# Two key tiles of an attention kernel written as one pattern of TensorE work

## The chip, the cores and the metric

The kernel runs on one core of a Trainium2 chip. The metric is the device time of one execution in microseconds. The kernel before took 3696.45 us in the median of three runs (3693.88 to 3697.93). All times below are in microseconds unless they are marked otherwise.

## What is computed

The reference is one transformer block with four batches of 2048 rows and 256 features, everything in float32. Attention has 16 heads of 16 features; the feed-forward part has 704 hidden features, and its activations and weights are quantized to FP4 in blocks of 16 and multiplied out again.

```
q, k, v = heads(x @ Wq.T), heads(x @ Wk.T), heads(x @ Wv.T)
scores  = einsum('bhld,bhmd->bhlm', q, k) * SCALE
out     = einsum('bhlm,bhmd->bhld', softmax(scores), v)
x = layernorm(x + merge(out) @ Wo.T)
h = silu(fp4(x) @ fp4(w_gate).T) * (fp4(x) @ fp4(w_up).T)
x = layernorm(x + fp4(h) @ fp4(w_down).T)
```

## The kernel before, in words

Attention is cut into 64 steps: batch, block of 512 queries (QB), and group of four heads (`steps`, line 351). A step walks over 16 tiles of 128 keys (NKT), and each such tile of one step is a period, so there are 1024 of them. The main loop (line 700) counts periods in `n`, with 20 more in front (LEAD) and 2 behind (LAG).

In one period the loop hands out this work, and `matmul` and `transpose` (lines 133 to 137) keep TensorE in the order in which it is written:

- `maxima` (line 382), for the step that is 20 periods ahead: for each pair of heads two matmuls of 62 rows into a two-bank PSUM tile `pm` (two buffers), then one VectorE reduction `mx` over both (line 397). They find the maximum of each query's scores, which the exponentials later subtract.
- `exponentials` (line 423), for the present step: for each pair of heads two matmuls `pe` of 64 rows, each into a bank from `psum` (line 106), then two ScalarE exponentials `e` (line 431). The even head lies on rows 0 to 63 of the array, the odd head on rows 64 to 127. The 64 rows are 16 features in a split of high and low parts, with two rows for the maximum.
- `values` (line 434), for the tile two periods back: four matmuls that the compiler makes into eight, `av`, 32 columns of the array for each head.
- `period` (line 654): it runs the steps that have fallen due (`take_due`, line 122), one part of each generator in `urgent`, and then parts of the first generator in `queue` until one with a cost of at least LEAST (300) has been run (two such parts before the first exponentials). A cost is a number that a generator yields; it serves to count parts alone.

The order in a period is: both maxima, first pair of exponentials, values, second pair of exponentials, then the part.

The banks that `psum` gives out are three, used in turn by the exponentials and by every part. `urgent` holds `max_rows` (line 399), which reduces the maxima of a finished step, pauses twice, transposes them (`pn`), copies them with ScalarE (`nr`) and has SyncE's queue write them into the last two rows of the query tiles with four DMAs (line 418); and `normalize` (line 448), which copies the finished `av` with ScalarE, pauses twice, transposes it (`pa`), divides it, and for every second step transposes the result (`pr`). `queue` holds everything else in parts: the projections of the next batch (`project`, line 300, tiles `ptx`, `pq`, `pv`), the quantized weights (`prepare`, line 232), and for each finished query block `chain` (line 673) with `feed_forward` (line 585): `residual` (`py`), `gated` (`pg`, `pu`), `turned` (`pth`) and `down` (`pz`). A generator that has to wait for something yields LEAST without any work, and the part of that period is empty.

Loads of keys, queries and values (`load_k`, `load_q`, `load_v`, lines 354 to 380) go through SyncE's queue. Keys are loaded in blocks of 512 keys, two tiles per block, seven blocks ahead of the exponentials, into 20 buffers (line 369).

When the main loop is over, `banks["more"]` lets `psum` use the banks of the maxima as well, and the rest of the queue runs with one part in each `period` (line 739).

Of the kernel before, what the change touches and what calls it, by code (L numbers as in the profile page):

```python
# [28 lines left out]
F32 = mybir.dt.float32  # L32
F32R = mybir.dt.float32r
# [5 lines left out]
P = 128  # L39
# [12 lines left out]
LN_EPS = 1e-5  # L52
LEAD = 20
LAG = 2
LEAST = 300.0
PSUM = bass.MemoryType.PSUM
DRAM = bass.MemoryType.DRAM
# [16 lines left out]
def block_kernel(  # L74
# [58 lines left out]
    def matmul(*args, **kw):  # L133
        tc.keep_in_program_order(nc.tensor.matmul(*args, **kw))  # L134
# [97 lines left out]
    def prepare():  # L232

        raw = p2.tile([P, KC, D], F32, tag="wl", name="wo", bufs=1)
        nc.sync.dma_start(raw, wo.rearrange("(c p) k -> p c k", p=P))
        yield 0
        pt = psum("ptw")
        for kc in range(KC):
            for n in range(KC):
                at = (kc * KC + n) * P  # L240
                transpose(pt[:, at : at + P], raw[:, n, kc * P : (kc + 1) * P], ident)
        nc.scalar.copy(woT.rearrange("p k n -> p (k n)"), pt)
        yield 500

        def load(w, i):
            if w is w_down:
                t = p2.tile([P, FF], F32, tag="wl", name="wl", bufs=1)
                nc.sync.dma_start(t, w[i * P : (i + 1) * P, :])
                return fp4(p2, t.rearrange("p (b f) -> p b f", f=FB), "h")
            t = p2.tile([RF, 2, D], F32, tag="wl", name="wl", bufs=1)  # L250
            nc.sync.dma_start(t, w[2 * i * RF : 2 * (i + 1) * RF, :].rearrange("(c p) k -> p c k", p=RF))
            return fp4(p2, t.rearrange("p c (b f) -> p (c b) f", f=FB), "")

        def transposed(w, i, q, done):
            while not done():
                yield LEAST
            if w is w_down:
                q = q.rearrange("p b f -> p (b f)")
                for c0 in range(0, NFC, 4):
                    pt = psum("ptw")  # L260
                    for c in range(c0, min(c0 + 4, NFC)):
                        n = min(P, FF - c * P)
                        at = (c - c0) * P
                        transpose(pt[:n, at : at + P], q[:, c * P : c * P + n], ident)
                        nc.scalar.copy(wdT[:n, c, i * P : (i + 1) * P], pt[:n, at : at + P])
                return
            q = q.rearrange("p (c b) f -> p c (b f)", c=2)
            pt = psum("ptw")
            for kc in range(KC):
                for c in range(2):  # L270
                    at = (2 * kc + c) * RF
                    transpose(pt[:, at : at + RF], q[:, c, kc * P : (kc + 1) * P], ident[:RF, :RF])
            dst = wgT if w is w_gate else wuT
            nc.scalar.copy(
                dst[:, :, 2 * i * RF : 2 * (i + 1) * RF], pt[:, : 4 * RF].rearrange("p (k n) -> p k n", k=KC)
            )

        pieces = [(w, i) for w in (w_gate, w_up) for i in range(4)] + [(w_down, i) for i in range(KC)]
        q = load(*pieces[0])
        yield 1  # L280
        for piece, after in zip(pieces, pieces[1:] + [None]):
            following = load(*after) if after else None
            yield from transposed(*piece, *q)
            q = following
            yield 500

    def weave(main, other, k):

# [11 lines left out]
    def project(b, tb, what):  # L300
# [7 lines left out]
        for kc in range(KC):  # L308
            pt = psum("ptx")
            for t in range(QT):  # L310
                transpose(pt[:, t * P : (t + 1) * P], xb[:, t, kc * P : (kc + 1) * P], ident)
            nc.scalar.copy(xT[:, kc, :], pt)
            yield 600
        for name, c in [(w[0], int(w[1])) for w in what if w != "v"]:
            w, dst = (wkT, kx[b % 2][c][:, :, rows]) if name == "k" else (wqT, qx[(b * NQB + tb) % len(qx)][c])
            hi = p2.tile([P, QB], F32R, tag="hi", name=name + "hi", bufs=3)
# [48 lines left out]
    def load_k(s, kb):  # L365
        b, qb, g = steps[s]
        for i in range(NP):
            c, h = divmod(g * HG + i * 2, NC)
            k = p1.tile([P, QB], F32R, tag="k", name="k", bufs=20)
            for j in range(2):  # L370
                nc.sync.dma_start(
                    k[R * j : R * j + R, :].bitcast(F32), kx[b % 2][c][:, h + j, kb * QB : (kb + 1) * QB]
                )
            k_sb[s, i, kb] = k
# [45 lines left out]
                )  # L420
        yield 400

    def exponentials(s, kt, i):
        kb, col = kt // QT, kt % QT * P
        pe = [psum("pe") for _ in range(2)]
        for j in range(2):
            rows = slice(R * j, R * j + R)
            matmul(pe[j], k_sb[s, i, kb][rows, col : col + P], q_sb[s, i][rows, :], start=True, stop=True)
        for j in range(2):
            e = p1.tile([P, QB], F32, tag="e", name="e", bufs=10)  # L430
            nc.scalar.activation(e, pe[j], AF.Exp, scale=SCALE)  # L431
            e_sb[s, kt, 2 * i + j] = e

    def values(s, kt):
        if kt == 0:
# [12 lines left out]
    def normalize(s):  # L448

        av_sb = p2.tile([P, QB], F32, tag="av_sb", name="av_sb", bufs=1)  # L450
        nc.scalar.copy(av_sb, av_ps.pop(s))
        yield 0
        yield 0
        pa = psum("pa")
        for t in range(QT):
            transpose(pa[:, t * P : (t + 1) * P], av_sb[:, t * P : (t + 1) * P], ident)

        pairs = pa.rearrange("p (t i a d) -> p t i a d", t=QT, i=NP, d=DH)
        rd = p2.tile([P, QT, NP, 2], F32, tag="rd", name="rd")
        nc.vector.reciprocal(rd, pairs[:, :, :, 1:3, 0])  # L460
        if s % 2 == 0:
            oq_of[s // 2] = p2.tile([P, QT, P], F32, tag="oq", name="oq", bufs=1)
        oq = oq_of[s // 2].rearrange("p t (g i j d) -> p t g i j d", g=2, i=NP, d=DH)
        for i in range(NP):
            nc.vector.tensor_tensor(
                oq[:, :, s % 2, i],
                pairs[:, :, i, 0:4:3, :],
                rd[:, :, i, :].unsqueeze(3).to_broadcast([P, QT, 2, DH]),
                ALU.mult,
            )  # L470
        yield 500
        if s % 2 == 0:
            return
        yield 0
        pr = psum("pr")
        for t in range(QT):
            transpose(pr[:, t * P : (t + 1) * P], oq_of[s // 2][:, t, :], ident)
        oT = p1.tile([P, QB], F32, tag="oT", name="oT", bufs=3)
        nc.scalar.copy(oT, pr)
        oTs[s // 2] = oT  # L480
        yield 500


    def layer_norm(r, t0, n):
# [69 lines left out]
    def turned(hq, tiles, hT):  # L554
# [4 lines left out]
        for t in range(2):  # L559
            pt = psum("pth")  # L560
            for c in range(4):
                transpose(pt[:, c * P : (c + 1) * P], hq[t][:, c * P : (c + 1) * P], ident)
            nc.scalar.copy(hT[:, t, :4, :].rearrange("p c n -> p (c n)"), pt)
            yield 500
        pt = psum("pth").rearrange("p (t c n) -> p t c n", t=2, c=2)
        for t in range(2):
            for c in range(4, NFC):
# [2 lines left out]
        for c in range(4, NFC):  # L570
            w = min(P, FF - c * P)
            nc.scalar.copy(hT[:w, :, c, :], pt[:w, :, c - 4, :])
        yield 500

    def down(x1, hT, t):
        for n in range(KC):
# [8 lines left out]
    def feed_forward(b, qb, between):  # L585
# [14 lines left out]
        for kc in range(KC):  # L600
            pt = psum("ptq")
            for t in range(QT):
                q = xq[t // 2][0].rearrange("p (t b) f -> p t (b f)", t=2)
                transpose(pt[:, t * P : (t + 1) * P], q[:, t % 2, kc * P : (kc + 1) * P], ident)
            nc.scalar.copy(xqT[:, kc, :], pt)
            yield 500
        hq = {}

        def gate(t):
# [41 lines left out]
                q.popleft()  # L651
        return None

    def period(parts):

        take_due()
        for _ in range(len(urgent)):
            cost = next(urgent[0], None)
            if cost is not None:
# [1 line left out]
            urgent.popleft()  # L661
            parts -= (cost or 0.0) >= LEAST
        while parts > 0 and queue:
            parts -= (part(queue) or 0.0) >= LEAST

    def projection(b, tb, what=("k0", "q0", "v", "k1", "q1")):
        return project(b, tb, what)
# [29 lines left out]
    others = [projection(0, tb, ("q0", "q1")) for tb in range(1, NQB)] + [projection(1, 0)]  # L697
    queue.append(weave(prepare(), chain_of(others), 2))

    for n in range(-LEAD, N + LAG):  # L700
        m = n + LEAD
        (sm, im), (s, kt), (sv, kv) = divmod(m, NKT), divmod(n, NKT), divmod(n - LAG, NKT)
        if m in (8, 10, 12, 14):
            if m == 8:
                load_q(1)
# [13 lines left out]
                assert (b, kb // QT, "k" + c) in projected  # L719
                load_k(ahead, kb // QT)  # L720

        for i in range(NP):
            if m < N:
                maxima(sm, im, i)
        for i in range(NP):
            if 0 <= n < N:
                exponentials(s, kt, i)
            if i == 0 and n >= LAG:
                values(sv, kv)
        if m < N and im == NKT - 1:  # L730
            urgent.append(max_rows(sm))
        if n >= LAG and kv == NKT - 1:
            urgent.append(normalize(sv))
            if sv % NG == NG - 1:
                queue.append(chain(*steps[sv][:2]))
        period(1 if n >= 0 else 2)
    banks["more"] = True
    while urgent or queue or due:
        period(1)

# [1 line left out]
_INS = [  # L744
    "L0_attn_x",
# [29 lines left out]
```

## Time and profile before

The profile is that of one execution, which took 3695.37 us by its own measurement; its span, from the first instruction to the last, is 3693.6 us. That lies 1.1 us under the median of the runs.

| what | value |
|---|---|
| median of three runs | 3696.45 us |
| the profiled execution's own time | 3695.37 us |
| its span | 3693.6 us |
| mean granted TensorE clock | 0.982 |
| `mx` reductions on VectorE | 2048, busy 2407.9 us, mean 1217 ns |
| `e` exponentials on ScalarE | 4096, busy 2217.9 us, mean 595 ns |
| `av` matmuls | 8192, busy 1098.3 us |
| `pe` matmuls | 4096, busy 1037.2 us |
| `pm` matmuls | 4096, busy 803.8 us |
| ScalarE idle before `e`, waiting for `pe` | 666.0 us |
| VectorE idle before `mx`, waiting for `pm` | 702.5 us |

A row of the profile names the engine, the line of the kernel, the operation, the tile that is written and those that are read, and how often it was executed. PE is TensorE's matmul, PEld its weight load, DVE is VectorE, ACT ScalarE, POOL GpSimd, and SPq SyncE's DMA queue. The timeline gives start, length and operation; instructions of one kind that follow each other are merged into one row. [...] lengths overlap and the distance of two starts says more. Behind `<-` stands what ended the idle time before a row.

### The profile page before, as it was taken

How to read it: one execution, taken by the hardware profiler on the slowest of the kernel's cores; microseconds unless marked ns; L12 is line 12 of the kernel's file. 1: busy time of each engine (PE TensorE's matmuls, PEld its weight loads, DVE VectorE, ACT ScalarE, POOL GpSimd, SP SyncE). 2: the span in 40 equal slices, each digit the busy share in tenths (PEclk: the TensorE clock that was granted, in tenths of full speed). 3: DMA queues.
4: the chain of work that ended last, by engine and by line, in shares of the span. 5: the costliest groups of instructions: out<-in, count | busy, mean ns of one | idle time of the engine just before them, and what ended most of it. 6: DMA issues, size and time to landing. Idle time of an engine off the chain costs nothing.

```text
span 3693.6 us, 57860 instructions
## 1 busy us (share of the span) xinstructions
PE 3540.7 (96%) x21396; PEld 1602.0 (43%) x21396; DVE 2805.0 (76%) x3250; ACT 2694.0 (73%) x5452; POOL 1293.4 (35%) x1542
## 2 busy tenths in 40 slices
PE   5889999999999999999999999999999999999995
PEld 4433444444444444444444444444443434444343
DVE  3777777787787877878787787778778788878834
ACT  2667777777777777777777777777777777777772
POOL 0331432424243242423424243342424325241425
PEclk8899999999999999999999999999999999999997
DMA  6643333223232332323323232322322221222100
GB/s 217 188 137 117 93 91 105 81 85 115 68 114 84 94 94 85 109 70 109 95 78 106 85 97 88 97 89 74 113 75 63 75 79 57 75 68 86 47 7 6
DMA packets 197954, 334.18 MB, mean 90 GB/s; under 512 B 26024, under 2 KB 75560, under 8 KB 197672
## 3 DMA queue, kind: packets, MB, share of 16 engines
q1 hardware_dynamic: 196280, 329.16, 29.2%
q8 instruction: 171, 2.80, 0.3%
q10 hardware_dynamic: 1392, 1.31, 0.1%
q14 instruction: 111, 0.91, 0.1%
HBM read 242.81 MB, written 86.51 MB: 89 GB/s over the span
## 4 chain that ended last, share of the span: by engine, by line
PE 82%; DVE 11%; DMA 2%; POOL 2%; SPq 1%; issue 1%; ACT 1%; ACTq 0%; POOLq 0%; DVEq 0%
PE av L134 24%; PE pe L134 18%; PE pm L134 16%; DVE mx L397 8%; PE pz L134 5%; PE pg L134 5%; PE pu L134 5%; PE pq L134 3%; PE pth L137 1%; PE pv L134 1%; PE pa L137 1%; PE py L134 1%; PE pn L137 1%; DMA k<-kx 1%; DMA xb<-in_L_attn_x_dram 1%; DVE amax L149 1%
## 5 line engine op out<-in xcount | busy, mean ns | idle before, releaser
L397 DVE TENSOR_REDUCE mx<-pm 128x2 f32<-128x1024 f32 x2048 | 2407.9, 1217 | 706.8 <-PE pm L134 702.5
L431 ACT ACTIVATE e<-pe 128x512 f32<-128x512 f32 x4096 | 2217.9, 595 | 671.2 <-PE pe L134 666.0
L134 PE MATMUL av<-e,v 128*32 128x512 f32 x8192 | 1098.3, 608 | 0.0
L134 PE MATMUL pe<-q,k 64*128 64x512 f32 x4096 | 1037.2, 456 | 4.8 <-ACT e L431 4.4
L134 PEld LDWEIGHTS pe<-q,k 64*128 64x128 f32 x4096 | 476.4, 185 | 969.0 <-ACT e L431 855.7
L134 PE MATMUL pm<-k,q 62*128 62x512 f32 x4096 | 803.8, 448 | 60.0 <-DVE mx L397 53.0
L134 PEld LDWEIGHTS pm<-k,q 62*128 62x128 f32 x4096 | 347.0, 186 | 373.2 <-issue 178.6
L134 PEld LDWEIGHTS av<-e,v 128*32 128x32 f32 x8192 | 162.2, 108 | 332.2 <-issue 314.1
L537 POOL TENSOR_TENSOR a<-a,g 128x352 f32<-128x352 f32 x124 | 116.4, 939 | 499.5 <-ACT a L536 499.5
L582 POOL TENSOR_TENSOR x<-x,read 128x128 f32<-128x128 f32 x128 | 58.9, 460 | 493.6 <-ACT read L142 493.6
L134 PE MATMUL pz<-wdT,hT 128*128 128x128 f32 (+1 forms) x1536 | 230.0, 292 | 0.0
L163 POOL TENSOR_TENSOR xn<-xn,m 128x704 f32<-128x704 f32 (+2 forms) x104 | 159.5, 1534 | 157.7 <-DVE m L162 139.0
L134 PEld LDWEIGHTS pz<-wdT,hT 128*128 128x128 f32 (+1 forms) x1536 | 191.0, 191 | 45.5 <-ACT e L431 18.2
L551 POOL TENSOR_TENSOR h<-a,u 128x352 f32<-128x352 f32 x124 | 116.2, 937 | 226.7 <-ACT u L550 224.4
L134 PE MATMUL pg<-wgT,xqT 128*128 128x352 f32 x512 | 187.4, 489 | 0.0
L513 POOL TENSOR_TENSOR x<-x,read 128x256 f32<-128x256 f32 x64 | 46.7, 730 | 400.2 <-ACT read L142 399.9
L134 PE MATMUL pu<-wuT,xqT 128*128 128x352 f32 x512 | 186.1, 486 | 0.0
L164 POOL TENSOR_TENSOR xn<-xn,m 128x704 f32<-128x704 f32 (+2 forms) x104 | 159.8, 1536 | 5.6
L165 POOL TENSOR_TENSOR xn<-xn,sc 128x704 f32<-128x704 f32 (+2 forms) x104 | 131.5, 1264 | 7.8
L538 POOL TENSOR_TENSOR a<-a,g 128x352 f32<-128x352 f32 x124 | 118.8, 958 | 9.7
L134 PEld LDWEIGHTS pg<-wgT,xqT 128*128 128x128 f32 x512 | 88.3, 191 | 58.5 <-ACT e L431 19.1
L134 PEld LDWEIGHTS pu<-wuT,xqT 128*128 128x128 f32 x512 | 88.2, 191 | 58.7 <-ACT e L431 20.0
(95 smaller groups left out, 2283.1 us busy)
## 6 DMA issues: line engine op xcount, KB each, us to landing
k<-kx SPq DMA_DIRECT2D x1024, 128.0 KB
v<-vx SPq DMA_DIRECT2D x64, 768.0 KB
q<-qx SPq DMA_DIRECT2D x256, 124.0 KB
kx<-khi SPq DMA_DIRECT2D x64, 256.0 KB
qx<-qhi SPq DMA_DIRECT2D x64, 256.0 KB
xb<-in_L_attn_x_dram SPq DMA_DIRECT2D x27, 512.0 KB
vx<-vt SPq DMA_DIRECT2D x128, 96.0 KB
x<-in_L_attn_x_dram SPq DMA_DIRECT2D x16, 512.0 KB
```

Source lines behind the costliest of these rows:

```text
L134: tc.keep_in_program_order(nc.tensor.matmul(*args, **kw))
L137: tc.keep_in_program_order(nc.tensor.transpose(*args))
L163: engine.tensor_tensor(xn, xn, m, ALU.add)
L164: engine.tensor_tensor(xn, xn, m, ALU.subtract)
L165: engine.tensor_tensor(xn, xn, sc.unsqueeze(2).to_broadcast([p, nb, FB]), ALU.mult)
L397: nc.vector.tensor_reduce(mx_sb[s][:, t, 2 * i : 2 * i + 2, kb], pm, AX.X, ALU.max)
L431: nc.scalar.activation(e, pe[j], AF.Exp, scale=SCALE)
L513: nc.gpsimd.tensor_add(x1[:, t, :], x1[:, t, :], read(py[:, :D]))
L537: engine.tensor_mul(a, a, g)
L538: engine.tensor_add(a, a, g)
L551: engine.tensor_mul(h[:, cols], a, u)
L582: nc.gpsimd.tensor_add(x1[:, t, cols], x1[:, t, cols], read(pz))
```

## The change

Two periods become one pattern, which is written out as a list of steps. `m0 m1` and `n0 n1` are the maxima of the first and of the second period, `e0` to `e3` and `f0` to `f3` the exponentials of the four heads in each, one head at a time, `v` and `w` the values; `q` runs two parts one after the other, and `r` the rest of them, where `q` has stopped early. `q` stops after a part whose cost is exactly TIED (500): these are the last transposes ahead of matmuls that read what ScalarE copies out of them. All other costs of 500 become 600, which counts the same.

`exponentials` works on one head in place of a pair. Keys have 16 buffers in place of 20, exponentials 12 in place of 10. `max_rows` and `normalize` run their first part at once, where they are created (`begin`), and one further part with every `q`, which comes once in two periods; `normalize` has one pause less. The loads at the head of the loop body move into `loads(n)`, which is called ahead of `m0` and of `n0`, as is `take_due`. Before the first exponentials `r` runs two parts as well.

The core of the diff:

```
+ORDER = "m0 e0 m1 e1 q e2 n0 e3 v n1 f0 f1 r f2 w f3".split()
+TIED = 500.0
...
-            yield 600
+            yield TIED if kc == KC - 1 else 600
...
-            k = p1.tile([P, QB], F32R, tag="k", name="k", bufs=20)
+            k = p1.tile([P, QB], F32R, tag="k", name="k", bufs=16)
...
-    def exponentials(s, kt, i):
+    def exponentials(s, kt, h):
+        i, j = divmod(h, 2)
         kb, col = kt // QT, kt % QT * P
-        pe = [psum("pe") for _ in range(2)]
-        for j in range(2):
-            rows = slice(R * j, R * j + R)
-            matmul(pe[j], k_sb[s, i, kb][rows, col : col + P], q_sb[s, i][rows, :], start=True, stop=True)
-        for j in range(2):
-            e = p1.tile([P, QB], F32, tag="e", name="e", bufs=10)
-            nc.scalar.activation(e, pe[j], AF.Exp, scale=SCALE)
-            e_sb[s, kt, 2 * i + j] = e
+        pe = psum("pe")
+        rows = slice(R * j, R * j + R)
+        matmul(pe, k_sb[s, i, kb][rows, col : col + P], q_sb[s, i][rows, :], start=True, stop=True)
+        e = p1.tile([P, QB], F32, tag="e", name="e", bufs=12)
+        nc.scalar.activation(e, pe, AF.Exp, scale=SCALE)
+        e_sb[s, kt, h] = e
...
-        yield 500
+        yield 600
         if s % 2 == 0:
             return
-        yield 0
         pr = psum("pr")
...
-    def period(parts):
-
-        take_due()
+    def more(parts):
+
         for _ in range(len(urgent)):
             cost = next(urgent[0], None)
...
         while parts > 0 and queue:
-            parts -= (part(queue) or 0.0) >= LEAST
+            cost = part(queue) or 0.0
+            parts -= cost >= LEAST
+            if cost == TIED:
+                break
+        return parts
...
+    def begin(urgently):
+        next(urgently)
+        urgent.append(urgently)
+
+    for n in range(-LEAD, N + LAG, 2):
+        left = 0
+        for step in ORDER:
+            n_of = n + (step[0] in "nfwr")
+            m = n_of + LEAD
+            if step in ("m0", "n0"):
+                loads(n_of)
+                take_due()
+            if step[0] in "mn" and m < N:
+                maxima(*divmod(m, NKT), int(step[1]))
+                if step == "n1" and (m + 1) % NKT == 0:
+                    begin(max_rows(m // NKT))
+            elif step[0] in "ef" and 0 <= n < N:
+                exponentials(*divmod(n_of, NKT), int(step[1]))
+            elif step in "vw" and n >= LAG:
+                s, kt = divmod(n_of - LAG, NKT)
+                values(s, kt)
+                if kt == NKT - 1:
+                    begin(normalize(s))
+                    if s % NG == NG - 1:
+                        queue.append(chain(*steps[s][:2]))
+            elif step == "q":
+                left = more(2)
+            elif step == "r" and n < 0:
+                more(2)
+            elif step == "r":
+                while left > 0 and queue:
+                    left -= (part(queue) or 0.0) >= LEAST
     banks["more"] = True
     while urgent or queue or due:
-        period(1)
+        take_due()
+        more(1)
```

The same marking with TIED is made at the last transposes of `xqT` in `feed_forward` (line 606) and at the last ones of `turned` (line 573).

More of the change, by code (lines that the diff above doesn't have):

```diff
@@ L284, in prepare @@
             q = following
-            yield 500
+            yield 600
     def weave(main, other, k):
@@ L470, in normalize @@
             )
-        yield 500
+        yield 600
         if s % 2 == 0:
             return
-        yield 0
         pr = psum("pr")
@@ L480, in normalize @@
         oTs[s // 2] = oT
-        yield 500
+        yield 600
     def layer_norm(r, t0, n):
@@ L563, in turned @@
             nc.scalar.copy(hT[:, t, :4, :].rearrange("p c n -> p (c n)"), pt)
-            yield 500
+            yield 600
         pt = psum("pth").rearrange("p (t c n) -> p t c n", t=2, c=2)
@@ L572, in turned @@
             nc.scalar.copy(hT[:w, :, c, :], pt[:w, :, c - 4, :])
-        yield 500
+        yield TIED
     def down(x1, hT, t):
@@ L605, in feed_forward @@
             nc.scalar.copy(xqT[:, kc, :], pt)
-            yield 500
+            yield TIED if kc == KC - 1 else 600
         hq = {}
@@ L698, in block_kernel, with loads @@
     queue.append(weave(prepare(), chain_of(others), 2))
-    for n in range(-LEAD, N + LAG):
+    def loads(n):
         m = n + LEAD
-        (sm, im), (s, kt), (sv, kv) = divmod(m, NKT), divmod(n, NKT), divmod(n - LAG, NKT)
+        s, kt = divmod(n, NKT)
         if m in (8, 10, 12, 14):
@@ L720, in block_kernel @@
                 load_k(ahead, kb // QT)
[L722 to L736, printed above, removed]
+    def begin(urgently):
[29 more added lines that the diff above has]
+                    left -= (part(queue) or 0.0) >= LEAST
     banks["more"] = True
     while urgent or queue or due:
-        period(1)
+        take_due()
+        more(1)
 _INS = [
```

## The prediction

> **What bounds the kernel now.** I read the page first (busy shares, then the chain that ended last), then the waits of TensorE, then TensorE's timeline in a stretch from the steady part.
>
> ```profile
> span 3693.6 us, 57860 instructions
> PE 3540.7 (96%) x21396; PEld 1602.0 (43%) x21396; DVE 2805.0 (76%) x3250; ACT 2694.0 (73%) x5452; POOL 1293.4 (35%) x1542
> PE 82%; DVE 11%; DMA 2%; POOL 2%; SPq 1%; issue 1%; ACT 1%; ACTq 0%; POOLq 0%; DVEq 0%
> ```
>
> TensorE is busy 96% and carries 82% of the chain, so only what changes TensorE's own stream, or makes it wait, moves the end. The waits view puts just 53.0 us of TensorE's time on DVE's row maxima and 4.4 us on ACT's exponentials. What, then, is inside the 96%? The timeline (start, length, operation; [...] I take start to start):
>
> ```profile
> 1517.50 0.50 PE L134 MATMUL pe<-q,k 64*128 64x512 f32 x2
> 1517.93 1.45 PE L134 MATMUL pu<-wuT,xqT 128*128 128x352 f32 x4
> 1519.31 0.73 PE L134 MATMUL pm<-k,q 62*128 62x512 f32 x4
> 1519.88 0.40 PE L134 MATMUL pe<-q,k 64*128 64x512 f32 x2
> 1520.20 1.07 PE L134 MATMUL av<-e,v 128*32 128x512 f32 x8
> 1521.20 0.50 PE L134 MATMUL pe<-q,k 64*128 64x512 f32 x2
> ```
>
> A period is four stretches of different array shapes. A lone pair of scores takes 1517.93-1517.50 = 0.43; the stretch of three pairs (two pm, one pe) 1520.20-1519.31 = 0.89. So one pair more costs (0.89-0.43)/2 = 0.23, and each stretch of scores has 0.20 that is no work. The values take 1.00. The part pu takes 1.38 alone; in the tail, where parts follow each other, one takes 3634.81-3633.63 = 1.18, so a part, too, has 0.20 that goes when another part stands before it:
>
> ```profile
> 3633.63 1.35 PE L134 MATMUL pu<-wuT,xqT 128*128 128x352 f32 x4
> 3634.81 1.35 PE L134 MATMUL pg<-wgT,xqT 128*128 128x352 f32 x4
> ```
>
> The sum 0.43+1.38+0.89+1.00 = 3.70 is the period (1521.20-1517.50). Nothing waits in it: the boundaries are the bound.
>
> [...] 0.20 at each change of shape, 0.23 a pair inside one. [...] The last two pz of a part have 64 rows and stand ahead of the maxima in the program:
>
> ```profile
> 1625.38 1.69 PE L134 MATMUL pz<-wdT,hT 128*128 128x128 f32 x11
> 1626.71 0.50 PE L134 MATMUL pm<-k,q 62*128 62x512 f32 x1
> 1626.91 0.27 PE L134 MATMUL pz<-wdT,hT 64*128 64x128 f32 x1
> 1626.94 0.71 PE L134 MATMUL pm<-k,q 62*128 62x512 f32 x3
> ```
>
> A pm (it must be the second head's, on the other 64 rows) starts at 1626.71, before the last pz at 1626.91, which comes earlier in the program. So each half of the rows runs its own line, at least two instructions ahead. [...]
>
> **The change part by part** (against the profiled run: span 3693.6, time 3695.4; the median 3696.45 is 1.1 above).
>
> *Scores.* Call the halves a (even heads) and b (odd). Between the boundaries the new order is: f3 m0 e0 m1 e1, then e2 n0 e3, then n1 f0 f1 f2. The first has m0a, e0, m1a on a and f3, m0b, m1b, e1 on b: 4 steps. The second has e2, n0a | n0b, e3: 2 steps, if n0b may start beside e2. The third has n1a, f0, f2 | n1b, f1: 3. So 9 steps and 3 boundaries, 9x0.23+3x0.20 = 2.67, against 8x0.23+4x0.20 = 2.64 for two periods now: +0.03. The saved boundary pays for the lost pairing, no more.
>
> *Parts in a row.* Two parts now cost 2x1.38, then 1.38+1.18: -0.20. Transposes behind a part save about 0.15 (steps of 0.11 inside, 0.17 and 0.20 at their ends). pz is the exception: its 64-row end now runs beside the maxima. Four pz in the tail (rows at 3666.46 and 3673.27) take 6.81/4 = 1.70 each, while alone it costs 3.85 (its period) - 2.32 = 1.54: +0.16 where pz goes first.
>
> *Counting one query block* (64 periods, 32 patterns). Its queue holds 60 parts and 4 periods stay empty (the timeline from 2331 to 2550). Laid out two at a time, 27 patterns get two in a row, two are split by TIED (the second goes to r, between f1 and f2: no boundary saved, +0.23 for the ninth step), two hold one, one none. Parts: 20x(-0.20)+4x(-0.15)+3x0.16 = -4.12. Scores: 27x0.03+2x0.23 = +1.27.
>
> *Waits that the change adds.* (1) Score banks are three, in turn, so the first part takes the bank of f3. f3's exponential starts 0.53 behind its matmul and lasts 0.60 (rows of ACT), and TensorE follows the end of an exponential after 0.05 (the empty periods at 3586): 1.18. The first stretch is over at 0.43+3x0.23 = 1.11. So TensorE waits 0.07, and everything behind it in its queue too: 30x0.07 = +2.1. Bounds: 0 if ACT's order leaves it free, 0.15 if ACT runs late. (2) A transpose as first part is short, and the next needs e0's bank: 0 to 0.05, 12 times: +0.3. (3) The copy of av is now ahead of f3's exponential on ACT: 0 to 0.33, three times where a part follows: +0.5.
>
> *Waits it takes away.* Empty periods take 2.6 to 2.75 now, though TensorE has only 0.20+4x0.23+1.00 = 2.12 of work: pairs need two banks at once. In the new order a walk through the three banks gives 5.1 for a pattern without parts (DVE's four maxima alone 4x1.18 = 4.7), and about 6.2 and 5.3 for those with one (now 6.55 and 5.88): together -1.1. The two periods behind the residual (4.19 and 3.73, against 3.09 and 3.39) wait for DVE, which computes a burst between maxima; with maxima in four places some of that is hidden: -0.5 (0 to -1.4).
>
> Sum: -4.12+1.27+2.1+0.3+0.5-1.1-0.5 = -1.55 per block, 16 blocks: **-25 us**.
>
> *At nothing.* 16 buffers for k in place of 20: SP's loads wait until f3 of the period before is done (they were free 8 periods earlier); stores of the projection, q and nr stand behind them. Four issues take 5 us at most (a row of x4 at 1501 has 4.98) and the next nr is over 7 us later; the keys are needed 8 periods (29 us) on. 12 buffers for e are exactly what is alive at v. max_rows: its reduction starts at once, but its two pauses are patterns now, so pn comes with the pattern before e0. From pn to e0 there were at least 6.2 us without a wait on q; now part 2 (1.06 to 1.7), two score stretches, two v and 0.33: 5.4 to 6.0. Two of its DMAs are issued 2.9 after pn[...]. Bounds 0 and, if they land at 6.2, 0.5x64 = 34 us; I take 0. normalize: same count, pr in the same period as now, so the feed-forward starts no later. Start (372 us with empty periods and waits on DMA) and tail (95 us, one part at a time as now): 0, ±15. The new costs 600 for 500 only keep TIED unique.
>
> **Rivals.**
> - *Order (slower).* [...] n0b waits behind e2, the second stretch has 3 steps: 32x0.23x16 = +118: 3789. [...] against it the pz rows. It decides if n0's first matmul starts a step after e2 on both halves.
> - *Banks (slower).* The wait for f3's bank is larger since ACT has a queue in front of it. Each 0.05 costs 30x16x0.05 = 24; beyond 0.12 the gain is gone, at 0.2 it is +62: 3733. For it: 0.07 is already out of three tight numbers; against it: ACT is idle a quarter of the time.
> - *Rows late.* The nr DMAs land at the upper bound: +34: 3704, no change.
> - *No wait.* f3's bank is free in time: -34 more: 3637.
>
> **How the numbers follow.** Likeliest: 3696.45-25 = 3671, chance 0.43 (its own range 3650 to 3692). No wait 0.18, banks 0.17, order 0.12, rows late 0.10. The range leaves out order and little else: 3635 to 3755. A difference of 0.2% (7.4 us) is about what a measurement of this kernel tells from none. Faster: 0.40 of the likeliest, 0.16 of no wait: 0.56. Same: 0.18 (the edge of the likeliest, rows late, part of banks). Slower: 0.26.
>
> **What would show it.** In a pattern with two gate parts, about 7.30 from f3 to f3 (7.40 now). pg to pu 1.18 apart. n0's first matmul beside e2, the stretch e2 n0 e3 0.66 long. Waits: a first part on ACT's e of some 30 us in all, none of pe on q's DMA, the 53 us of pm on DVE smaller. It would be wrong if the three score stretches hold 10 steps, or if the first part waits 0.12 or more.

## The result, and the profile after

The changed kernel took 3827.19 us in the median of four runs (3821.99 to 3828.52), the kernel before 3695.49 beside it (3693.88 to 3697.93): the ratio is 1.0352, with a 95% interval of 1.0336 to 1.0367. I had predicted 3671. The profiled execution took 3826.83, with a span of 3825.0.

The head of the page after, in the same three lines as before:

```profile
span 3825.0 us, 58032 instructions
PE 3584.2 (94%) x21396; PEld 1658.2 (43%) x21396; DVE 2838.6 (74%) x3250; ACT 2651.3 (69%) x5452; POOL 1300.0 (34%) x1542
PE 72%; DVE 13%; POOL 6%; ACT 4%; issue 2%; DMA 2%; SPq 0%; POOLq 0%; ACTq 0%; DVEq 0%
```

Each of the five engines of the second line executes as many instructions as before. TensorE's share of the chain fell from 82% to 72%, and what came in is GpSimd, 2% to 6%, and ScalarE, 1% to 4%. Nothing in the change touches GpSimd. So the first question is who waits for it. VectorE's waits in the kernel before and then after (total us, times, longest):

```profile
DVE st L489 <- POOL x L582: 30.0, 6, 8.0
DVE amax L149 <- POOL h L551: 17.1, 2, 15.3
DVE amax L149 <- POOL x L497: 4.1, 2, 2.2
```

```profile
DVE st L492 <- POOL x L585: 96.6, 62, 8.0
DVE amax L154 <- POOL h L554: 50.7, 36, 14.8
DVE amax L154 <- POOL x L500: 39.2, 32, 2.2
```

A wait that came twice now comes 32 times, twice in each of the 16 blocks. TensorE's own waits after:

```profile
PE pm L139 <- DVE mx L402: 108.9, 102, 5.8
...
PE pe L139 <- DVE oq L469: 11.3, 41, 0.5
```

The wait for the row maxima doubled (53.0 before), where I had it smaller. Yet most of the new pattern came out as laid out. Here is TensorE's timeline, in which a pattern begins with the row `pe ... x1` at 1797.43 and the next at 1804.74:

```profile
1797.43 0.49 PE L139 MATMUL pe<-q,k 64*128 64x512 f32 x1
...
1798.62 1.45 PE L139 MATMUL pu<-wuT,xqT 128*128 128x352 f32 x4
1799.90 1.35 PE L139 MATMUL pg<-wgT,xqT 128*128 128x352 f32 x4
1801.18 0.49 PE L139 MATMUL pe<-q,k 64*128 64x512 f32 x1
...
1801.85 1.06 PE L139 MATMUL av<-e,v 128*32 128x512 f32 x8
...
1804.74 0.50 PE L139 MATMUL pe<-q,k 64*128 64x512 f32 x1
```

`pu` is 1.45 long and `pg` starts 1.28 behind it, so I go from start to start. The first stretch of scores takes 1798.62-1797.43 = 1.19, the two parts `pu` and `pg` 2.56, the second stretch 1801.85-1801.18 = 0.67, and the whole pattern 7.31.

I cut all traces at the first `py` of each query block and added up, start to start, what lies in parts, in scores and in values (mean of eight full blocks, us):

| kernel | block | parts | scores | values |
|---|---|---|---|---|
| before | 218.6 | 61.5 | 93.4 | 63.8 |
| after | 226.9 | 60.5 | 101.8 | 64.6 |
| after, pinned (e3 below) | 220.7 | 59.3 | 97.7 | 63.8 |

Over all eleven full blocks the kernel after is 8.1 longer in each, 89 us in all; the last four, which have no projection in their queue, add 37 (10.7, 10.3, 10.4 and 5.1), the start 5 and the end 1.

**Where 6 of the 8.3 are.** The FP4 rounding of the residual's rows begins on VectorE with `amax`, the maximum of each group of 16; `sc` and `rs` follow, its scale and the reciprocal; GpSimd multiplies (`xn`), and VectorE makes a mask `m` that GpSimd rounds with. VectorE's timeline at one residual of the kernel after:

```profile
2212.32 1.21 DVE L402 TENSOR_REDUCE mx<-pm 128x2 f32<-128x1024 f32 x1
2214.64 0.69 DVE L154 TENSOR_REDUCE amax<-x 128x32 f32<-128x512 f32 x1 [1.12 <-POOL x L500]
2215.25 0.21 DVE L407 TENSOR_REDUCE nm<-mx 128x16 f32<-128x64 f32 x1
2215.37 0.51 DVE L156 TENSOR_SCALAR sc<-amax 128x32 f32<-128x32 f32 x1
...
2216.19 1.03 DVE L410 TENSOR_TENSOR nh<-nm,nh 128x16 fp32r<-128x16 f32 x1
2217.14 3.48 DVE L402 TENSOR_REDUCE mx<-pm 128x2 f32<-128x1024 f32 x3
```

and TensorE's at the same place:

```profile
2214.89 0.49 PE L139 MATMUL pe<-q,k 64*128 64x512 f32 x1
2218.40 0.50 PE L139 MATMUL pm<-k,q 62*128 62x512 f32 x2 [3.02 <-DVE mx L402]
2218.74 0.40 PE L139 MATMUL pe<-q,k 64*128 64x512 f32 x1
2219.07 1.93 PE L139 MATMUL av<-e,v 128*32 128x512 f32 x8
2220.93 0.79 PE L139 MATMUL pm<-k,q 62*128 62x512 f32 x2
```

The FP4 maximum `amax` stands in VectorE's queue ahead of three `mx`. It waits 1.12 for GpSimd's layer norm (`x L500`), then `sc`, `rs` and the first part of `max_rows` (`nm`, `nh`) run, and the first `mx` starts at 2217.14. TensorE has two buffers for `pm`, both full, so it stands for 3.02. The other half of the same residual, 11 us earlier, costs it 1.42 in the same way. There, too, VectorE keeps to the order of its queue: an `mx` whose matmuls were over at 2203.64 (`pm` at 2203.14, 0.50 long) starts at 2205.91, right behind such an `amax`, though VectorE has stood idle for 1.24.

The third cost shows in the busy table by stretch (length; busy time of PE, PEld, DVE, ACT and POOL; granted clock; DMA):

```profile
2214.90:2218.40 3.50, 0.48 (x2) 0.17 (x1) 3.50 (x8) 1.18 (x3) 3.26 (x3) 1.00 0.76 215
2218.40:2223.40 5.00, 5.00 (x20) 1.94 (x20) 3.81 (x5) 1.68 (x3) 1.27 (x2) 0.66 0.00 0
```

For 5 us behind the stop TensorE's granted clock is 0.66, and the eight `av` take 2220.93-2219.07 = 1.86 in place of 1.00: at 0.66 the 5.0 us are worth 3.3, so by this estimate 1.7 are lost. 1.4 + 3.0 + 1.7 = 6.1 make the 6. Cut at every second group of eight `av`, the four patterns around these two stops take 33.7 in the mean of the eight blocks, 27.7 in the kernel before and 27.6 with the order of VectorE repaired (e3 below).

### The profile page after: what moved, and what is told of

Same layout as the page of the kernel before. It is cut to its first block, busy times and chain, and to the rows that moved or that the text cites. A ratio compares the mean times of both kernels' runs of the same rounds, so it can differ in the third digit from the quotient of the medians.

```text
span 3825.0 us, 58032 instructions
## 1 busy us (share of the span) xinstructions
PE 3584.2 (94%) x21396; PEld 1658.2 (43%) x21396; DVE 2838.6 (74%) x3250; ACT 2651.3 (69%) x5452; POOL 1300.0 (34%) x1542
## 4 chain that ended last, share of the span: by engine, by line
PE 72%; DVE 13%; POOL 6%; ACT 4%; issue 2%; DMA 2%; SPq 0%; POOLq 0%; ACTq 0%; DVEq 0%
PE av L139 22%; PE pe L139 17%; PE pm L139 12%; DVE mx L402 8%; PE pz L139 5%; PE pu L139 3%; PE pg L139 3%; PE pq L139 3%; ACT e L435 3%; PE pth L142 1%; DVE amax L154 1%; PE pv L139 1%; PE py L139 1%; POOL x L500 1%; PE pn L142 1%
## 5 line engine op out<-in xcount | busy, mean ns | idle before, releaser
L402 DVE TENSOR_REDUCE mx<-pm 128x2 f32<-128x1024 f32 x2048 | 2437.5, 1217 | 670.0 <-PE pe L139 452.7
L435 ACT ACTIVATE e<-pe 128x512 f32<-128x512 f32 x4096 | 2193.7, 603 | 612.1 <-PE pe L139 570.9
L139 PE MATMUL pe<-q,k 64*128 64x512 f32 x4096 | 1320.3, 427 | 16.8 <-DVE oq L469 11.3
L139 PE MATMUL pm<-k,q 62*128 62x512 f32 x4096 | 1142.5, 458 | 116.6 <-DVE mx L402 108.9
L139 PEld LDWEIGHTS pe<-q,k 64*128 64x128 f32 x4096 | 614.3, 188 | 689.9 <-ACT e L435 484.5
L139 PEld LDWEIGHTS pm<-k,q 62*128 62x128 f32 x4096 | 489.8, 187 | 639.7 <-DVE mx L402 266.2
L540 POOL TENSOR_TENSOR a<-a,g 128x352 f32<-128x352 f32 x124 | 116.2, 937 | 500.5 <-ACT a L539 500.5
L147 ACT COPY read<-pz 128x128 f32<-128x128 f32 x128 | 33.9, 265 | 151.4 <-PE pm L139 88.1
L492 DVE BATCH_NORM_STATS2 st<-x 128x6 f32<-128x256 f32 x128 | 54.3, 424 | 111.2 <-POOL x L585 96.6
L537 ACT COPY g<-pg 128x352 f32<-128x352 f32 x128 | 57.9, 452 | 98.7 <-PE pg L139 96.6
```

The source lines that it names most:

```text
L402: nc.vector.tensor_reduce(mx_sb[s][:, t, 2 * i : 2 * i + 2, kb], pm, AX.X, ALU.max)
L435: nc.scalar.activation(e, pe, AF.Exp, scale=SCALE)
L492: nc.vector.bn_stats(st, r[:, t0 + t, :])
L537: nc.scalar.copy(g, pg[:, :FH])
L540: engine.tensor_mul(a, a, g)
```

## Experiments

Theory **Queue**: the loss is the place of VectorE's GpSimd-dependent operations among the row maxima. The code orders TensorE by hand (`keep_in_program_order`); on VectorE the scheduler may draw an operation ahead of others. Rival: the pattern itself costs more on TensorE than I had laid out (banks, empty patterns).

**e1 and e2: no wait for x.** The residual's `amax` is taken of `wqT`, which is long finished, in the kernel after (e1) and before (e2); the scale is then not that of x.

```
-        nc.vector.tensor_reduce(amax, t, AX.X, ALU.max, apply_absolute_value=True)
+        nc.vector.tensor_reduce(amax, t if seen is None else seen, AX.X, ALU.max, apply_absolute_value=True)
```

> The changed kernel, with the block maxima of the residual's FP4 step read from a weight tile that is never rewritten, in place of the layer-normed rows: same instruction, same size, no wait for GpSimd; the quantized values are therefore not the reference's. Theory Q (VectorE's queue stands at these maxima until GpSimd has normalized the rows, row maxima of the scores stand behind them, and TensorE runs out of score buffers, some 7 us in each of 16 query blocks, half of it idle and the rest a slower clock after it): about 3827 - 16 x 6.5 = 3723, and the waits of pm on mx fall from 108.9 us to under 60. Theory S (the pattern itself is dearer: single heads lose their pairing): within 20 us of 3827.

> The kernel before with the same substitution (quantized values not the reference's). Theory Q: there the maxima are hardly waited for (4.1 us in all), so 3696 - 0 to 20. Theory S: the same as Q here; the run is the measure against which the first is read: if both fall by the same amount, the substitution and not the removed wait is the cause.

Measured: e1 3841.20 (1.0389, 1.0365 to 1.0413), e2 3764.89 (1.0177, 1.0160 to 1.0194). Both missed. The wait did not go, it moved down the same queue: in e1 the mask `m` waits for GpSimd's `xn` 81.0 us in place of 28.3, and `pm` for `mx` 118.5. But e2 is telling: the kernel before loses 65 us too, though no operation is added and only what `amax` reads has changed, and with it when it can run (`pm` for `mx` 100.7 in place of 53.0, `m` for `xn` 40.2 in place of 12.9).

**e3: one instruction kept in its place** in the kernel after; `pinned` is set by the residual alone.

```
-        nc.vector.tensor_reduce(amax, t, AX.X, ALU.max, apply_absolute_value=True)
+        seen = nc.vector.tensor_reduce(amax, t, AX.X, ALU.max, apply_absolute_value=True)
+        if pinned:
+            tc.keep_in_program_order(seen)
```

> The changed kernel with one line more: the maxima of the residual's FP4 step are pinned behind everything that is already written for VectorE, so that they cannot be drawn ahead of the row maxima of scores written before them. Nothing is left out. Theory Q: most of the stall goes, 3827 - 16 x 5 = 3747 (range 3720 to 3770). Theory S: no change.

Measured: 3752.58, ratio 1.0145 (1.0130 to 1.0160): 75 us of the 131 are gone. `pm` waits 67.9 us, the mean clock is 0.983 (0.972 in the kernel after). This is what Queue had. None of the 32 waits of `amax` for `x` is left. At the same place of another block `amax` now runs without a wait, and single `mx` stand around it:

```profile
1948.85 0.68 DVE L154 TENSOR_REDUCE amax<-x 128x32 f32<-128x512 f32 x1
1949.44 1.22 DVE L404 TENSOR_REDUCE mx<-pm 128x2 f32<-128x1024 f32 x1
1950.57 1.17 DVE L158 TENSOR_SCALAR sc<-amax 128x32 f32<-128x32 f32 x1
```

**e4: the residual one part at a time**, in the kernel after: `yield TIED` for `yield 900`.

> The changed kernel with the four residual parts of a query block marked TIED, so that no two of them, nor one of them and the next part, run in a row: the second goes to r. This undoes parts in a row for 2 to 3 patterns of 32. Cost by the prediction's own terms: 3 x 0.43 x 16 = +21 us. Theory Q: the two layer norms get further apart and some of the stall goes, 3827 + 21 - 60 = 3790 (range 3750 to 3830). Theory S: 3827 + 21 = 3848.

Measured: 3801.98 (1.0277, 1.0261 to 1.0292), as expected: the residual one part at a time takes off 25 us, a third of what the order does.

**e5: the same pin in the kernel before.**

> The kernel before with the same pin on the residual's maxima that took 75 us from the changed kernel. Queue theory (the change lost its 75 us because its two-period order let the scheduler draw these maxima ahead of row maxima that were ready; the kernel before was spared most of it, with 1.4 us a block at most there): 3690, range 3675 to 3705, TensorE's wait of pm for mx stays near 53 us. Rival (the pin helps any order, and the change has no part in the loss): 3625.

Measured: 3700.09 (1.0007, 0.9999 to 1.0016), `pm` for `mx` 61.8. The pin as such brings nothing; the change had brought the bad order.

**e6: all such operations pinned** in the kernel after (every `amax`, the layer norms' `st`, the masks `m`).

> The changed kernel with every maximum, every first step of a layer norm and every mask of a rounding kept in its place on VectorE. Queue theory: what VectorE still waits for GpSimd in the kernel with one pin (st 96 us, amax<-h 50, m 47) holds up row maxima now and then, so pm's wait for mx falls from 67.9 to some 50 and the time from 3752.6 to 3735, range 3715 to 3750. Rival (what is left is not in VectorE's order): 3752, within 5.

Measured: 3741.35 (1.0121, 1.0106 to 1.0136), `pm` for `mx` 44.1, less than before the change. Eleven more, but not in the full blocks, which stay at 220.8: the start is 19 shorter than in e3 and the last four blocks together 8 longer. Against the kernel before, e6 has 25 more in the eleven full blocks, 35 more in the last four and 13 less in the start. The kernel before with all these pins was not run, so whether its start would gain as much is not shown.

**e7 and e8: each half of the change alone.** e7 has single heads but one part at `q` and one at `r`, with e3's pin. e8 is the kernel before with its pairs and the same pin, and has two parts in every other period; its next period has none.

```
-                left = more(2)
+                left = more(1)
...
-                while left > 0 and queue:
-                    left -= (part(queue) or 0.0) >= LEAST
+                more(1)
```

```
-        period(1 if n >= 0 else 2)
+        left = period(2 if n < 0 or n % 2 == 0 else left)
```

> The pinned changed kernel with one part at q and one at r, so that no two parts follow each other and the single heads have four stretches of scores (the f2 behind r stands alone). By the stretches of the trace a full pattern then has one boundary more in the scores and one more at the parts, 0.40 in all; 25 of these a block are 10, less some 4 for the waits that two parts in a row bring (f3's bank, py for oT, transposes that saved less): plus 6 a block, 96 in all: 3850, range 3810 to 3880. Rival (parts in a row give nothing, since waits take the place of the boundaries): 3750, within 15.

> The kernel before with the pin, its pairs kept, and both parts of two periods in a row in the first of them; the second has none. Without waits a pattern would lose two boundaries, 0.40, about 27 times a block: 3520. Banks theory: the four pairs that then follow each other need two banks at a time, and this costs what an empty period shows, 2.60 in place of 2.12, so plus 0.48 against minus 0.40: 3730, range 3690 to 3780. Rival (the wait for two banks is hidden since the exponentials have caught up during two parts): 3560, range 3520 to 3620.

Measured: e7 3953.87 (1.0692, 1.0674 to 1.0710), 201 above e3, more than either theory; e8 3923.97 (1.0615, 1.0598 to 1.0631), 224 above e5. So the row of parts is worth more than I had, and each half alone loses far more than both together. In e7 a block's scores are 7.4 longer than in e3 in 27 stretches more, its parts 4.0; some of it is waiting that came with it (`pm` for `mx` 96.5 in place of 67.9). In e8 the period without a part is the loss, and what it waits for is not the score banks that I had named but the two buffers of the maxima (215.4 in all, 61.8 in e5):

```profile
1738.37 0.39 PE L134 MATMUL pm<-k,q 62*128 62x512 f32 x2
1739.09 0.50 PE L134 MATMUL pm<-k,q 62*128 62x512 f32 x2 [0.33 <-DVE mx L399]
```

That half pattern has 1.71 of scores, where my stretches gave 1.12 without a wait.

**What is left of e6: three edits.** A pattern without parts takes 5.61 in e6, and its merged first stretch shows a wait for an exponential and a late `pm`:

```profile
1894.46 0.40 PE L139 MATMUL pe<-q,k 64*128 64x512 f32 x1
1895.13 0.50 PE L139 MATMUL pe<-q,k 64*128 64x512 f32 x1 [0.28 <-ACT e L435]
1895.70 0.50 PE L139 MATMUL pm<-k,q 62*128 62x512 f32 x2
```

*e9* puts the values there (all later runs have e6's pins):

```
+                before = banks["n"]
                 left = more(2)
+                if banks["n"] == before and n >= LAG:
+                    order.remove("v")
+                    order.appendleft("v")
```

> The changed kernel with all pins (3741.4); where the step q finds no part that gives TensorE work, the values (step v) come right there, between e1 and e2, so that an empty pattern is f3 m0 e0 m1 e1 | v | e2 n0 e3 n1 f0 f1 f2 | w. An empty pattern takes 5.61 in the trace, 2.71 of it in the merged first two stretches, where n0 waits for the maxima of m0 and e2 for a bank. Empty-pattern theory (this is one of the terms that my walk had wrong): with the values between them the waits are covered and the pattern falls to some 4.8, that is 0.8 once or twice in a full block and 7 times or more in the last four: about minus 37, 3704, range 3690 to 3720. Rival (VectorE's four maxima, 4x1.18 and what else it has, set an empty pattern in any order): 5.3 a pattern, 3725 or more.

Measured: 3728.80 (1.0084, 1.0067 to 1.0101), minus 13, close to the rival: an empty pattern now takes 5.24, two empty periods before took 2x2.61 = 5.22. A wait of 0.31 for VectorE's maxima stands in it. The change gains nothing from a pattern without parts.

The second place is the bank that `pa` holds until VectorE has written `oq`, here in the kernel after:

```profile
1791.37 0.66 PE L142 MATMUL pa<-ident,av_sb 128*128 128x128 f32 x4
1791.86 1.44 PE L139 MATMUL pg<-wgT,xqT 128*128 128x352 f32 x4
1793.24 0.50 PE L139 MATMUL pe<-q,k 64*128 64x512 f32 x1
1793.24 0.73 PE L139 MATMUL pm<-k,q 62*128 62x512 f32 x2
1794.14 0.47 PE L139 MATMUL pe<-q,k 64*128 64x512 f32 x1 [0.17 <-DVE oq L469]
1794.54 1.06 PE L139 MATMUL av<-e,v 128*32 128x512 f32 x8
```

The stretch takes 1794.54-1793.24 = 1.30 in place of 0.67. *e10* puts `pa` and `pr` behind the first part (`begin(normalize(s), second)`); *e11* has e9, e10 and no two `pz` in a row.

> The changed kernel with all pins; the transposes of normalize (pa, pr) come behind the first part from the queue and not ahead of it; values of the next step are loaded four periods later, since v is then projected a little later. Bank theory: pa's bank is held until VectorE's last multiplication to oq, and with pg behind it e3 is given that bank while oq is still being written (second stretch 1.30 in place of 0.67); and py right behind pr waits for oT (2.08 for 1.50). With pa last in the row the bank comes up one step later: some 0.5 three times a block, and 0.4 once for pr with py: minus 1.6 to 1.9 a block, 3714, range 3700 to 3730. Rival (the wait for oq moves on to f0, as in the pattern with pa alone, where the third stretch has 1.6): 3741, within 8.

> The changed kernel with all pins, values ahead in empty patterns, normalize behind a part, and two parts pz no longer in a row (their 64-row ends lay beside the maxima when alone: a pattern with two of them in a row takes 7.99, two periods before took 7.72). If the terms add up: 3741-37-27-5 = 3672, range 3655 to 3695, and the pattern of two parts in a row with single heads is then faster than the kernel before by what I had predicted. Rival (the waits only change places): 3710 to 3740.

Measured: e10 3754.00 (1.0150, 1.0135 to 1.0165), e11 3744.51 (1.0129, 1.0114 to 1.0144). Both missed. The bank came free in one place of three in a block (the stretch behind `pu` and `pa` takes 0.67, those behind `ptq` and `pa` and behind `pv` and `pa` 0.81 and 1.48), and the residual's parts now fell into other patterns, and in the block that I followed the mask, pinned ahead of an `mx`, waited 1.61 for GpSimd; TensorE stood for 1.44 and, 4 us later, for 1.49. From the second block to the last `py` e10 has 28 stops of TensorE over 0.9 us, e9 has 4. Splitting the two `pz` gave nothing.

*e12* starts the rounding one period later on top of e9, *e13* on top of e9 and e10, *e14* as e13, but `pr` ahead as before.

```
-        return xn, later(1, rounded, 4 if tag == "" else 2)
+        return xn, later(2 if tag == "" else 1, rounded, 3 if tag == "" else 2)
```

> All pins and values ahead (3728.8), and the residual's rounding starts two periods behind its scaling, not one, and is waited for three periods, not four, so that the transposes of xq come at the same place. Queue theory (the mask m, held in its place, keeps row maxima waiting for GpSimd's xn, 75.3 us of VectorE's time in 83 waits): most of these waits go, in the full blocks some 0.5 and in the last four, where two patterns behind the residual have stretches of 3.79 and 3.42 in place of 1.18 and 0.67 and then a slower TensorE, some 6: about minus 25, 3704, range 3690 to 3718. Rival (the stretches there are long since VectorE has too much to do in them, whatever it waits for): 3729, within 6.

> All pins, values ahead, all transposes of normalize behind a part (as in the run before that has all, without the change to pz), and the residual's rounding one period later. In the run with normalize behind, a full block had 1.44 and 1.49 of TensorE waiting for mx behind the residual, the first while VectorE waited 1.61 for xn ahead of the mask; that hid the gain of the freed bank. Queue theory: 1.5 to 3 a block come back: 3700, range 3685 to 3720. Rival (the bank gives nothing): 3729 or more.

> As the run with both and the mask later, but only pa comes behind a part; pr stays ahead of py, so that no slot of the queue is lost to the wait for oT. If the terms add up: 3704 of the run with the mask later, less 0.6 twice and 0.4 once a block for the bank: minus 20: 3684, range 3670 to 3705, and then faster than the kernel before. Rival (a new order on VectorE's queue brings a new wait): 3705 to 3740.

Measured: e12 3724.65 (1.0075, 1.0062 to 1.0089), not to be told from e9; e13 3723.59 (1.0067, 1.0051 to 1.0082), 30 below e10, of which e9's edit explains 13, if it gives the same here; the rest would be the mask; e14 3715.73 (1.0050, 1.0037 to 1.0062), 9 below e12 for `pa`'s bank, where I had 20: the two stretches behind `pg` and `pa` take 0.97 and 1.02, half-way from 1.30 to 0.67. e14 still ends above the kernel before.

**e15 to e17: without FP4.** The FP4 rounding is left out, on VectorE and, but for one copy, on GpSimd: in the kernel before (e15), in the kernel after (e16), and in the kernel after with e9's values and e14's `pa` (e17). e17 also keeps `st` in its place, which the other two don't.

> The kernel before without the FP4 rounding: every group of values goes on unrounded, by one copy on GpSimd, and VectorE's maxima, scales, reciprocals and masks of FP4 are left out, in the weights too. It is the base for the other two. By the waits of the kernel before (53.0 us of pm for mx, about half of it at the start and behind the residuals) it gains 20 to 40: 3665, range 3640 to 3685.

> The changed kernel without the FP4 rounding in the same way, with no pin. Queue theory (VectorE's FP4 work was the main loss, the bank of pa and the empty patterns the rest, some 30 to 45): the distance to the kernel before without FP4 falls from 131 to within 20, 3670, range 3650 to 3690. Rival (the loss is in TensorE's own order and the three banks): 50 or more above the other.

> The changed kernel without the FP4 rounding, with values ahead in empty patterns and pa behind a part. Stretch theory (without waits for VectorE and for pa's bank the patterns cost what my sum had): 25 to 40 below the kernel before without FP4: 3635, range 3620 to 3655. Rival (parts in a row and the lost pairs only balance): equal to it within 10.

Measured: 3619.41 (0.9788 of the full kernel before, 0.9773 to 0.9802), 3637.13 (0.9835, 0.9820 to 0.9850) and 3607.07 (0.9752, 0.9736 to 0.9769). e15 gains 79 where I had 20 to 40; 33 of them lie behind the last block's first `py` and 15 ahead of the first block. The distance of change to base is 18 in place of 131: 113 of the loss need the FP4 work (the runs don't part VectorE's from GpSimd's). With the reordering the change is 12 below its base, where e17's expectation had 25 to 40. In the full blocks, though, they are equal:

| kernel | block | parts | scores | values | first `py` at |
|---|---|---|---|---|---|
| e15, before | 217.15 | 61.14 | 92.25 | 63.76 | 359.8 |
| e17, after reordered | 217.15 | 59.84 | 93.55 | 63.76 | 349.5 |

The 12 are 10 in the start and 0.5 in each of three of the last blocks. The start may be the pin's doing: e16, which has none, is only 4 ahead of e15 there. So even without the FP4 work the pattern balances in the steady part, and the gain that I had forecast there is not found.

## Why the prediction was wrong, by its own steps

**The step that failed** is "the two periods behind the residual", in *Waits it takes away*: "with maxima in four places some of that is hidden: -0.5 (0 to -1.4)". It came out at plus 6 a full block (33.7 in place of 27.7 in the four patterns). I treated VectorE's burst as work to be hidden, and did not ask in what order VectorE would stand: nothing in the code fixes it, and a new order of TensorE's program gave a new one. e3 shows it (minus 75 for one pinned instruction, the four patterns back at 27.6), e2 shows that the kernel before had the same weakness, and e5 that it was not suffering from it. "At nothing" should have had a line for it; my range ended at 3755, and none of my rivals was this one.

With that repaired the sum would still have failed: the terms below turn -1.55 into about +2.6 a block, and e6's full blocks are 2.2 longer than those before. I also counted 16 equal blocks. The last four have no projection and so more patterns without parts; in e6 these four alone add 35 us.

**Parts in a row**, predicted -4.12. There are 27 rows of two, as I had counted. Two matmul parts save 0.20 (2.56, 1.92, 2.24), as said; a part and then transposes save 0.14. Wrong was transposes *ahead* of a matmul part, eight rows with `pa`, `pr` or `pn`: 0.04 to 0.10 (`pa` and `pg` 1.87 against 0.59+1.38), but once 0.19. `pr` ahead of `py` costs 0.43 more than the two alone, since `py` waits for the `oT` that ScalarE is copying: the very thing that TIED avoids elsewhere. `pz` was right: two in a row take 3.05, and 0.20 of a tail beside the scores, against 2x1.53, so +0.19 where I had +0.16. Row by row the parts of e6, `pz`'s tails included, add up to some -2.5, so this term was 1.6 too large.

**Scores**, +1.27, and **the first part's wait**, +2.1: right. Nine steps and three boundaries; stretches of 1.18 to 1.19 (predicted 1.18 with the wait), 0.67 (0.66) and 0.90. Order, the rival, which no row of before had spoken for, is out: n0 does start beside e2 (its first `pm` at 1801.19, e2 at 1801.18; a second stretch of 0.67 is two steps, three would be 0.89), as it would if each half of the rows runs its own line.

**Left out** of the waits: `pa`'s bank, 0.63 twice and some 0.36 once in a block. I had priced when a bank is asked for, not that `pa`'s is held by three VectorE operations which queue behind maxima.

**Empty patterns**, -1.1: some -0.2. The pattern without parts and the two with one take 5.61, 6.27 and 5.60 in e6, where I had walked the three score banks to 5.1, 6.2 and 5.3; the first of them is longer than the two empty periods before (5.22). For this one the walk left out the two `pm` buffers (e8, e9); in the one with `pa` it is `pa`'s bank again.

**At nothing**: that `pn`'s copies by DMA would be in time was my estimate, as no row of before shows when they land. They were (no wait for q among TensorE's waits), and so were the keys with 16 buffers: `pm` waits once for them, for 5.9 us, where it waited once for 5.3 before.

What each edit took off the 3827.19:

| edit | us | taken off |
|---|---|---|
| residual's `amax` pinned (e3) | 3752.6 | 75 |
| all pinned (e6; intervals overlap) | 3741.4 | 11 |
| values ahead in empty patterns (e9) | 3728.8 | 13 |
| mask later (e12; not told apart) | 3724.7 | 4 |
| `pa` behind a part (e14; the interval touches e12's) | 3715.7 | 9 |

Open: the last 18 us of e14. Its start is 14 shorter than that of the kernel before, its eleven full blocks are 17 longer together, and its last four also 17. Without FP4 a full block has 3.0 less (e17); 1.4 of that is one stretch of scores behind the residual, 2.55 long in place of 1.18, where the mask has waited 0.67 for GpSimd and `pm` then waits twice for `mx`. In each of the last four blocks of e14's trace TensorE stops once for 1.32 behind the residual, and then has a granted clock of 0.50 for 6.8 us. So much of what e14 loses belongs to the FP4 work; to place each of its steps by hand was not tried, and what the pins would give the kernel before is open too.

## What to carry to other kernels

When one engine's order is written by hand and another's is left to a scheduler, a change to the first was here also a change to the second (one instruction put back in its place gave 75 of 131 us, e3): look in the new order for operations that wait for a third engine and stand ahead of what feeds the bound engine, and price the wait with all that is queued behind it. Where parts are put in a row, the saving here was 0.20 for two matmul parts, while `pr` ahead of `py` cost 0.43 and a second `pz` 0.19; ask for each pair whether the second reads what the first's copy still has to deliver, and how long the first holds its bank. Two halves of a change can each lose far more alone than together (e7 201 above e3, e8 224 above e5), and a gain that does not appear (e10) may be hidden by a wait that has only moved.

## What I had not expected of the hardware

A stop of TensorE cost more here than its length. In the kernel after, from the second block to the last `py`, there are 14 stops between 1.94 and 3.08 us, and behind each the next eight `av` take 1.45 to 1.86 in place of 1.00; behind 17 stops of 1.14 to 1.42 they take 1.00 fourteen times and 1.09, 1.20 and 1.76 in the others. The granted clock goes with it: it is 0.50 for 3.4 or 6.8 us at every one of the 14, and for 3.4 us at five of the 17, among them the three with more than 1.00.
